# Where a scan leaves its result, and when its product with C is taken: a two-layer Mamba and expert block on one core

## The chip, the cores and the metric

The kernel runs on 1 core of one Trainium2 chip. The metric is the device time of one execution in microseconds; three executions before the change took 4998.74, 5000.21 and 5006.12 us, so the median is 5000.21 us. The profile is one further execution.

Five engines matter below: TensorE (PE; its weight loads are PEld), VectorE (DVE), ScalarE (ACT), GpSimd (POOL) and SyncE (SP), which here only issues DMAs. Each works through its own queue in order. SBUF and PSUM are the two memories on the core: TensorE writes to PSUM, the tiles of the loads lie in SBUF.

## The reference, cut to what matters

The input is (2, 256, 64, 64): two batches of 256 channels and 4096 positions. Layer 0 is a Mamba block over the positions, with 256 inner channels. Layer 1 is a layer norm, two Mamba blocks (one forward, one over the flipped sequence, 512 inner channels each), and then a mixture of 8 experts weighted by a softmax. The part that the change touches is the state recurrence, the same in all three Mamba blocks, with 16 states to a channel:

```python
A = -jnp.exp(A_log)
dA = jnp.exp(dt[..., None] * A)
dBu = dt[..., None] * Bm[:, :, None, :] * xs[..., None]
def combine(c1, c2):
    a1, b1 = c1
    a2, b2 = c2
    return (a1 * a2, a2 * b1 + b2)
_, hs = jax.lax.associative_scan(combine, (dA, dBu), axis=1)
y = jnp.einsum('blds,bls->bld', hs, Cm) + xs * Dvec
y = y * jax.nn.silu(z)
return y @ out_proj_w.T
```

For every channel and state, h(t) = dA(t) h(t-1) + dBu(t). The states are multiplied by C(t) and summed over the 16 states; the skip xs * D is added, and the gate silu(z) multiplies.

## The kernel before

**Tiling.** The 4096 positions are cut into chunks of T = 512. Six jobs (2 batches x layer 0, layer 1 forward, layer 1 flipped) of 8 chunks each run one after the other. In a chunk, each block of 128 channels is worked in 4 groups of states; one such group of one block is a *quad*: a tile `bq` of 128 partitions (32 channel rows x 4 states) by 4 x 512. There are 640 quads. `QN` = 8 quads make one *period*; `n` is the quad's place in it (0 to 7). A quad has two halves `h` = 0 and 1, each of 2 x 512 elements; one half is one *slot*, so a period has 16 slots and the whole has 1280.

**What a quad goes through.**
- `emit_b` (line 742, GpSimd): b = dt*x times B into `bq`, 128x2048. Both inputs, `rxdt` and `bc`, lie in SBUF. It is emitted some three quads ahead. `bq` has six buffers.
- `emit_decay` (line 752, ScalarE): the decays `da` = exp(dt*A) of one half into PSUM, two activations. `da` has two buffers. Ahead of it, `emit_join` (line 763) folds the carried state into the first column of the second row of b, so that one scan can run over both rows.
- `emit_scan` (line 778, VectorE): the scan over 1024 elements, with `da` and `bq` as inputs. Its result goes over `da` in PSUM, except where `on_pool(g, h)` holds: there it goes over `bq` in SBUF.
- The product with C. Where `on_pool` holds (quads 0, 2 and 5 of a period, and the first half of quad 4 in every second period) GpSimd does it: `emit_times_c_quad` (lines 802 and 803), after a small copy of the last column, in place on `bq`. Elsewhere, 760 of the 1280 halves, VectorE does it: `emit_times_c` (line 787), from `da` in PSUM and `bc` in SBUF into `bq`.
- `emit_carry` (line 797, ScalarE): copies the last column of each row into `h_state`, the state carried to the next chunk, in the halves that VectorE multiplies.
- `emit_sum` (line 811, TensorE): four matmuls add a quad's products over the states into `y` in PSUM; `emit_skip` (line 818) opens `y` with the skip, and `emit_gate` (line 824, VectorE) takes `y` times the gate. `y` has one buffer.

**Order.** The loop of lines 1105 to 1147 emits slot by slot, and `in_order` ties each engine to that order. `SUMS` (line 65) says in which slot which quads are summed; `POOL_AT` (line 66) which products GpSimd does at the start of which quad ("c0 b4" at n = 1: the product with C of quad 0, then b of quad 4, both counted from the period's start). In between stand the other steps of the chunks to come, which `Slots` holds by slot and queue: projections, convolution (line 544), softplus (line 594, and `xdt` on GpSimd, line 598), gate (line 624), layer norms, and the scales of the experts (lines 918 to 921, once).

**Experts.** `experts()` (line 927) plans ahead of time how many of the 128 pairs (16 chunks of the two batches with 8 experts each) fit into the slots of the scans, by a budget of TensorE's and ScalarE's work in each slot; `sums_in` tells it which slots the sums take. Those pairs (lines 992, 1001, 1005) leave their results in DRAM. The others run in a last stage after the scans (lines 1326, 1330, 1337, 1350), where the early results are also weighted and added (lines 1275, 1276).

The heart of the loop before the change:

```python
if slot:
    emit_carry(*divmod(slot - 1, 2))
emit_decay(*divmod(slot + 1, 2))
sl.run(slot, "act")
sl.run(slot, "dve0")
emit_scan(g, h)
if (n, h) in ((1, 0), (5, 0)) and done:
    emit_gate(*done.pop(0))
sl.run(slot, "dve")
if not on_pool(g, h):
    emit_times_c(g, h)
```

Of the kernel before, what the change touches and what calls it, by code (L numbers as in the profile page):

```python
# [50 lines left out]
T = 512  # L51
# [10 lines left out]

POOL_HALF = (4, 0)

SUMS = {(0, 0): (-1,), (2, 0): (0, 1), (4, 0): (2, 3), (6, 0): (4,), (7, 0): (5, 6)}
POOL_AT = {0: "b3", 1: "c0 b4", 2: "b5", 3: "c2 b6", 4: "b7", 5: "h4 b8", 6: "c5 b9", 7: "b10"}
HUGE = 1e37

# [68 lines left out]
def hybrid_kernel(ctx: ExitStack, tc: tile.TileContext, a: dict, out: bass.AP):  # L137
    nc = tc.nc
# [19 lines left out]
    def in_order():  # L158

        ins = nc.cur_bb.bb.instructions  # L160
        for x in ins[traced[0] :]:
            if x.engine in tail:
                tc.add_manual_dep(
                    x, tail[x.engine],
                    mybir.DependencyInfo(mybir.DependencyClass.NoSync, mybir.DependencyReason.DATA),
                    reason="in_order",
                )
            tail[x.engine] = x.name
        traced[0] = len(ins)
# [24 lines left out]
    with ExitStack() as st:  # L194
# [155 lines left out]
        steps = [(job, c) for job in jobs for c in range(NCH)]  # L350
# [318 lines left out]
        bq, da, y = {}, {}, {}  # L669
        pending, wanted = [], []  # L670

        def at(g):

            i, jp, n = quads[g]
            return i, 2 * jp + n // SG, n % SG
# [45 lines left out]
        def flush(slot):  # L721
            for p in list(pending):
                if p[0] <= slot and (p[1] if len(p[1]) > 1 else p[1][0]) in cks[p[3]]:
                    pending.remove(p)
                    p[2]()
# [42 lines left out]
        def on_pool(g, h):  # L768

            n = quads[g][2]  # L770
            return n in POOL_C or (n, h) == POOL_HALF and g // QN % 2

        def emit_scan(g, h):
            i, j, sg = at(g)
            job, c = steps[i]
            d = da[g, h].rearrange("p q t -> p (q t)")
            b = bq[g][:, 2 * h : 2 * h + 2, :].rearrange("p q t -> p (q t)")
            nc.vector.tensor_tensor_scan(  # L778
                b if on_pool(g, h) else d, d, b,
                job.h[:, j, sg, 2 * h : 2 * h + 1] if c else 0.0, ALU.mult, ALU.add,  # L780
            )

        def emit_times_c(g, h):

            i, j, sg = at(g)
            d, two = da[g, h], slice(2 * h, 2 * h + 2)
            nc.vector.tensor_tensor(  # L787
                bq[g][:, two, :], d,
                cks[i]["bc", 1, sg].rearrange("p (o t) -> p o t", o=1).to_broadcast([P, 2, T]), ALU.mult,
            )  # L790

        def emit_carry(g, h):

            i, j, sg = at(g)
            d, two = da.pop((g, h)), slice(2 * h, 2 * h + 2)
            if not on_pool(g, h):
                nc.scalar.copy(steps[i][0].h[:, j, sg, two], d[:, :, T - 1])  # L797

        def emit_times_c_quad(g, groups=SG):
            i, j, sg = at(g)  # L800
# [7 lines left out]
        def emit_sum(g):  # L808
            i, j, sg = at(g)
            for q in range(SG):  # L810
                nc.tensor.matmul(  # L811
                    y[i, j][q * CG : (q + 1) * CG, :], stack, bq[g][:, q, :],
                    start=False, stop=(sg == SG - 1),
                )

        def emit_skip(i, j):
            y[i, j] = ps_y.tile([P, T], F32, tag="y", name=f"y_{i}_{j}")
            nc.tensor.matmul(
                y[i, j], steps[i][0].diagonal[:, j, :], cks[i]["xc", j], start=True, stop=False
            )  # L820

        def emit_gate(i, j):
            sz = cks[i]["sz", j]
            nc.vector.scalar_tensor_tensor(sz, y.pop((i, j)), 0.5, sz, ALU.mult, ALU.mult)
# [102 lines left out]
        def experts():  # L927

            last = 2 * nq + 15
            banks = sorted(sl.banks, key=lambda r: r[0])  # L930

            def fits(slot):

                at = sum(b[0] <= slot for b in banks)
                both = banks[:at] + [(slot, slot + 1, 0)] + banks[at:]
                return all(
                    both[k - 3][1] + both[k][2] <= both[k][0] for k in range(max(3, at - 2), min(len(both), at + 4))
                    if at in range(k - 3, k + 1)
                )

            def sums_in(slot):
                n, h = divmod(slot % 16, 2)
                return 1.25 * len(SUMS.get((n, h), ())) + (1 if (n, h) in ((2, 0), (6, 0)) else 0)

            todo = [(at, b, c, e) for at, b, c in sorted(ready) for e in range(E)]
            behind = act_behind = 0.0
            times = [[], [], []]

            def follows(l):

                k, m = divmod(len(times[l]), KC)
                if k == len(todo):
                    return None
                waits = [(l - 1, k * KC + 1, 2)] if l else []
                if m:
                    waits.append((l, k * KC, 0))
                elif k:

                    waits.append((l, k * KC - 1, 6 if l == 0 and todo[k][-1] == 0 else 4))
                    if l < 2:  # L960
                        waits.append((l + 1, k * KC - 1, 0))
                if any(n >= len(times[w]) for w, n, _ in waits):
                    return None
                return max([todo[k][0] + 3] + [times[w][n] + d for w, n, d in waits])

            for slot in range(last):
                behind = max(0.0, behind) + sl.products.get(slot, 0) + sums_in(slot) - PE_ROOM
                act_behind = max(0.0, act_behind) + sl.acts.get(slot + 1, 0) - ACT_ROOM
                for l in (2, 1, 1, 0, 0):
                    at = follows(l)  # L970
                    if at is None or slot < at:
                        continue
                    if behind + 2 > PE_BEHIND or act_behind + 1.3 > ACT_BEHIND or not fits(slot):
                        break
                    banks.insert(sum(b[0] <= slot for b in banks), (slot, slot + 1, 0))
                    times[l].append(slot)
                    behind += 2
                    act_behind += 1 if l == 2 else 1.3
            put = [
                (*item[1:], [times[l][k * KC + m] for l in range(3) for m in range(KC)])  # L980
                for k, item in enumerate(todo) if (k + 1) * KC <= len(times[2])
            ]
            emit_experts(put)
# [120 lines left out]
        done = []  # L1104
        for g in range(nq):
            i, jp, n = quads[g]
            for h in range(2):
                slot = 2 * g + h
                sl.run(slot, "sp")
                flush(slot)  # L1110

                if (n, h) in ((2, 0), (6, 0)):
                    emit_skip(i, 2 * jp + n // SG)
                sl.run(slot, "pe")
                for m in SUMS.get((n, h), ()):
                    if g - n + m >= 0:
                        emit_sum(g - n + m)
                sl.run(slot, "pe2")
                if (n, h) in ((0, 0), (4, 0)) and g:
                    done.append(at(g - 1)[:2])  # L1120

                if slot:
# [4 lines that stand above are left out]
                sl.run(slot, "dve0")  # L1127
                emit_scan(g, h)

                if (n, h) in ((1, 0), (5, 0)) and done:  # L1130
                    emit_gate(*done.pop(0))
                sl.run(slot, "dve")
                if not on_pool(g, h):
                    emit_times_c(g, h)

                if h == 0:
                    for what in POOL_AT.get(n, "").split():
                        m = g - n + int(what[1:])
                        if what[0] == "c":
                            emit_times_c_quad(m)  # L1140
                        elif what[0] == "h":
                            if on_pool(m, 0):
                                emit_times_c_quad(m, SG // 2)
                        else:
                            want_b(m)
                sl.run(slot, "pool")
            in_order()
        emit_sum(g)
        emit_gate(i, steps[i][0].nj - 1)
        sl.run_all(2 * nq, 2 * nq + 24)  # L1150
# [3 lines left out]
    with ExitStack() as st:  # L1154
# [5 lines left out]
        n, x, y, acc, wts, wb, lt, w_dram = {}, {}, {}, {}, {}, {}, {}, {}  # L1160
# [278 lines left out]
        for at, (b, i, e) in enumerate(pairs):  # L1439
# [5 lines left out]
            h = layer(n[b, i], 0, e, f"{i}_{e}_{b}")  # L1445
# [136 lines left out]
```

## Time and profile before

| what | value |
|---|---|
| median of 3 executions | 5000.21 us |
| profiled execution, its own time | 5004.36 us |
| span of the profile | 5002.6 us |
| busy: PE | 4256.4 us (85%) |
| busy: VectorE | 4568.5 us (91%) |
| busy: ScalarE | 3617.3 us (72%) |
| busy: GpSimd | 4342.2 us (87%) |
| first scan to last scan | 58 to 4468 us |
| mean granted TensorE clock | 0.928 |

How to read it: the span is the time from the first to the last instruction of the profiled execution. Busy times are sums over instructions of one engine; engines overlap. The scans fill the first 4468 us; GpSimd has little to do after that. In rows of groups, a line of the kernel, an engine and an operation stand with "out<-in", the shape, the count, the summed busy time, the mean of one in ns, and the idle time just before them with what ended it. In the timeline a row has its start, its length, engine, line, operation and tiles. The scans write to `da` 760 times (664 with a carried state, 96 in first chunks) and to `bq` 520 times (456 and 64).

### The profile page before, as it was taken

The page shows a single profiled execution, that of the slowest core. Times are in us where ns is not written, and L with a number is a line of the kernel's source. Part 1 is how long each engine was busy: PE and PEld are TensorE (multiplying, and loading weights), DVE is VectorE, ACT ScalarE, POOL GpSimd, SP SyncE. Part 2 cuts the span into 40 slices and gives each one's busy share as a digit, 9 for nine tenths or more (in the row PEclk, how much of TensorE's full clock was granted, in tenths as well). Part 3 has the DMA queues.
Part 4 walks back from the last instruction along what each step waited for, and adds up shares of the span by engine and source line. Part 5 has one row for each costly group of instructions (what it writes and reads, how often), then busy time and mean ns, then how long its engine had stood idle before and what let it go on. Part 6 is the DMA issues. An engine that isn't in the chain of part 4 may idle for free. (4 is left out here: it accounts for less than half of the span.)

```text
span 5002.6 us, 47346 instructions
## 1 busy us (share of the span) xinstructions
PE 4256.4 (85%) x14912; PEld 1473.8 (29%) x14912; DVE 4568.5 (91%) x3097; ACT 3617.3 (72%) x7304; POOL 4342.2 (87%) x1424
## 2 busy tenths in 40 slices
PE   5777778778776899989999999889868999989999
PEld 1222222222222233333333333223222333334444
DVE  6998999999999999999999999999999999964655
ACT  5777777777777788877788788888767888862232
POOL 6998999999999999999999999999999999960000
PEclk8778899999887999999999999999989999999999
DMA  5455454444444555446776555555434455436643
GB/s 192 157 188 168 157 168 153 157 144 154 163 158 148 175 179 176 166 171 232 246 238 216 171 174 169 189 171 189 169 127 146 171 185 191 171 121 236 227 160 126
DMA packets 335408, 875.26 MB, mean 175 GB/s; under 512 B 36315, under 2 KB 111861, under 8 KB 293173
## 3 DMA queue, kind: packets, MB, share of 16 engines
q1 hardware_dynamic: 326164, 835.39, 48.3%
q0 software_dynamic: 8992, 36.85, 2.8%
q8 instruction: 118, 1.93, 0.2%
q14 instruction: 134, 1.09, 0.1%
HBM read 673.27 MB, written 198.84 MB: 174 GB/s over the span
## 5 line engine op out<-in xcount | busy, mean ns | idle before, releaser
L742 POOL TENSOR_TENSOR bq<-rxdt,bc 128x2048 f32<-128x2048 f32 x640 | 2894.3, 4545 | 15.7 <-DMA rxdt<-xdtd 7.7
L752 ACT ACTIVATE da<-rdt,w_a 128x512 f32<-128x512 f32 x2560 | 1756.9, 686 | 114.2 <-DVE bq L778 68.0
L778 DVE TENSOR_TENSOR_SCAN da<-da,h_state,bq 128x1024 f32<-128x1024 f32 x664 | 1558.0, 2346 | 60.4 <-ACT da L752 46.2
L803 POOL TENSOR_TENSOR bq<-bq,bc 128x2048 f32<-128x2048 f32 (+1 forms) x280 | 1180.4, 4216 | 22.6
L778 DVE TENSOR_TENSOR_SCAN bq<-da,h_state,bq 128x1024 f32<-128x1024 f32 x456 | 1059.7, 2338 | 22.0 <-ACT da L752 21.8
L811 PE MATMUL y<-bq,stack 128*32 128x512 f32 x5120 | 744.8, 667 | 254.3 <-POOL bq L803 229.5
L787 DVE TENSOR_TENSOR bq<-da,bc 128x1024 f32<-128x1024 f32 x760 | 926.4, 1219 | 15.7
L992 PE MATMUL e<-eh,ew 128*128 128x512 f32 x1376 | 669.8, 621 | 52.3 <-DVE sp L594 13.6
L797 ACT COPY h_state<-da 128x2 f32<-128x2 f32 x759 | 119.3, 157 | 631.6 <-DVE bq L787 628.3
L763 ACT ACTIVATE bq<-h_state,bq,a 128x1 f32<-128x1 f32 x1120 | 429.8, 384 | 2.9 <-POOL bq L742 2.3
L992 PEld LDWEIGHTS e<-eh,ew 128*128 128x128 f32 x1376 | 250.5, 194 | 466.5 <-issue 234.9
L458 PE MATMUL z<-nx,w_in 128*128 128x512 f32 x640 | 326.6, 639 | 62.5 <-DVE q L423 21.1
L811 PEld LDWEIGHTS y<-bq,stack 128*32 128x32 f32 x5120 | 140.7, 116 | 798.8 <-POOL bq L803 347.7
L531 PE MATMUL conv<-xs,w_conv 64*64 64x512 f32 x2560 | 346.6, 617 | 31.3 <-ACT xs L515 29.1
L992 PE MATMUL e<-en,ew 128*128 128x512 f32 x688 | 329.6, 612 | 26.9 <-DVE xr L891 16.1
L458 PE MATMUL xs<-nx,w_in 128*128 128x512 f32 x640 | 316.9, 622 | 34.7 <-DVE sz L624 20.7
L1330 ACT ACTIVATE h<-hp,of,sc 128x512 f32<-128x512 f32 x168 | 130.6, 778 | 277.5 <-PE hp L1326 274.7
L1005 ACT ACTIVATE eh<-e,of,sc 128x512 f32<-128x512 f32 x344 | 260.1, 769 | 53.9 <-PE e L992 53.6
L843 PE MATMUL o<-sz,w_out 128*128 128x512 f32 x640 | 295.7, 601 | 0.0
L598 POOL TENSOR_TENSOR xdt<-sp,xc 128x512 f32<-128x512 f32 x160 | 203.3, 1274 | 49.7 <-DVE sp L594 49.7
L778 DVE TENSOR_TENSOR_SCAN da<-da,bq 128x1024 f32<-128x1024 f32 x96 | 219.4, 2286 | 4.3 <-ACT da L752 2.3
L458 PEld LDWEIGHTS z<-nx,w_in 128*128 128x128 f32 x640 | 123.6, 202 | 266.3 <-issue 146.8
(145 smaller groups left out, 4762.3 us busy)
## 6 DMA issues: line engine op xcount, KB each, us to landing
rxdt<-xdtd SPq DMA_DIRECT2D x160, 1024.0 KB, 6.1
rdt<-dtd SPq DMA_DIRECT2D x160, 1024.0 KB, 6.8
bc<-bcd SPq DMA_DIRECT2D x384, 256.0 KB, 3.2
ew<-in_W SPq DMA_DIRECT2D x172, 256.0 KB, 4.5
u<-u SPq DMA_DIRECT2D x86, 512.0 KB, 5.7
u<-eu SPq DMA_DIRECT2D x82, 512.0 KB, 4.1
dtd<-sp SPq DMA_DIRECT2D x160, 256.0 KB, 3.3
xdtd<-xdt SPq DMA_DIRECT2D x160, 256.0 KB, 3.5
```

The lines of the kernel that those rows point to most:

```text
L458: nc.tensor.matmul(ps, job.matrices["in", half][:, k, j * P : (j + 1) * P], rhs, start=(k == 0), stop=(k == KC - 1),)
L531: nc.tensor.matmul(v[r][64 * col : 64 * col + 64, :], job.matrices["conv"][rows, 2 * jp + j, k, :], ck["xs", jp][rows, j, k : k + T] if k ...
L742: nc.gpsimd.tensor_tensor(bq[g], ck["rxdt", j], over_groups(ck["bc", 0, sg]), ALU.mult)
L752: nc.scalar.activation(da[g, h][:, k, :], cks[i]["rdt", j][:, q, :], AF.Exp, scale=steps[i][0].w["a"][:, j, q * SG + sg : q * SG + sg + 1],)
L763: nc.scalar.activation(bq[g][:, q, 0:1], job.h[:, j, sg, q : q + 1], AF.Identity, scale=cks[i]["a0", j][:, h, sg : sg + 1], bias=bq[g][:, ...
L778: nc.vector.tensor_tensor_scan(b if on_pool(g, h) else d, d, b, job.h[:, j, sg, 2 * h : 2 * h + 1] if c else 0.0, ALU.mult, ALU.add,)
L787: nc.vector.tensor_tensor(bq[g][:, two, :], d, cks[i]["bc", 1, sg].rearrange("p (o t) -> p o t", o=1).to_broadcast([P, 2, T]), ALU.mult,)
L803: nc.gpsimd.tensor_tensor(b, b, cks[i]["bc", 1, sg].rearrange("p (o t) -> p o t", o=1).to_broadcast([P, groups, T]), ALU.mult,)
L811: nc.tensor.matmul(y[i, j][q * CG : (q + 1) * CG, :], stack, bq[g][:, q, :], start=False, stop=(sg == SG - 1),)
L843: nc.tensor.matmul(v[m], job.w["out"][:, j, m * P : (m + 1) * P], ck["sz", j], start=False, stop=(j == job.nj - 1),)
L992: nc.tensor.matmul(ps, ew[l][:, k, m * P : (m + 1) * P], key[x][:, k, :], start=(k == 0), stop=(k == KC - 1),)
L1005: nc.scalar.activation(key[dst][:, m, :], key["ps", l, m], AF.Relu, bias=of[:, l, e, m : m + 1], scale=sc[:, l, e, m : m + 1],)
```

## The change

All scans write over b. In the 760 halves whose product with C belongs to VectorE, that product is now taken in place on `bq`, one slot later, behind the next scan; the carry copies from `bq`. Sums, skip and gate move by one slot, and so does what the planner of the experts is told of them.

```diff
-SUMS = {(0, 0): (-1,), (2, 0): (0, 1), (4, 0): (2, 3), (6, 0): (4,), (7, 0): (5, 6)}
+SUMS = {(0, 1): (-1,), (2, 1): (0, 1), (4, 1): (2, 3), (6, 1): (4,), (7, 1): (5, 6)}
...
             nc.vector.tensor_tensor_scan(
-                b if on_pool(g, h) else d, d, b,
+                b, d, b,
                 job.h[:, j, sg, 2 * h : 2 * h + 1] if c else 0.0, ALU.mult, ALU.add,
             )
...
         def emit_times_c(g, h):
             i, j, sg = at(g)
-            d, two = da[g, h], slice(2 * h, 2 * h + 2)
+            b = bq[g][:, 2 * h : 2 * h + 2, :]
             nc.vector.tensor_tensor(
-                bq[g][:, two, :], d,
+                b, b,
                 cks[i]["bc", 1, sg].rearrange("p (o t) -> p o t", o=1).to_broadcast([P, 2, T]), ALU.mult,
             )
         def emit_carry(g, h):
             i, j, sg = at(g)
-            d, two = da.pop((g, h)), slice(2 * h, 2 * h + 2)
+            two = slice(2 * h, 2 * h + 2)
             if not on_pool(g, h):
-                nc.scalar.copy(steps[i][0].h[:, j, sg, two], d[:, :, T - 1])
+                nc.scalar.copy(steps[i][0].h[:, j, sg, two], bq[g][:, two, T - 1])
...
-                return 1.25 * len(SUMS.get((n, h), ())) + (1 if (n, h) in ((2, 0), (6, 0)) else 0)
+                return 1.25 * len(SUMS.get((n, h), ())) + (1 if (n, h) in ((2, 1), (6, 1)) else 0)
...
-                if (n, h) in ((2, 0), (6, 0)):
+                if (n, h) in ((2, 1), (6, 1)):
                     emit_skip(i, 2 * jp + n // SG)
...
-                if (n, h) in ((0, 0), (4, 0)) and g:
+                if (n, h) in ((0, 1), (4, 1)) and g:
                     done.append(at(g - 1)[:2])
...
-                if (n, h) in ((1, 0), (5, 0)) and done:
+                if (n, h) in ((1, 1), (5, 1)) and done:
                     emit_gate(*done.pop(0))
                 sl.run(slot, "dve")
-                if not on_pool(g, h):
-                    emit_times_c(g, h)
+                if slot and not on_pool(*divmod(slot - 1, 2)):
+                    emit_times_c(*divmod(slot - 1, 2))
...
+        emit_carry(g, 1)
+        emit_times_c(g, 1)
         emit_sum(g)
```

## The prediction

> **What bounds the kernel now.** I read first where the time lies. The busy times of the stretch from the first scan to the last, 58 to 4468 us, and the page's costliest groups:
>
> ```profile
> 58.00:4468.00 4410.00, 3709.59 (x13528) 1237.31 (x13528) 4274.10 (x2782) 3441.57 (x7054) 4305.18 (x1375) 0.92 0.51 174
> ...
> L742 POOL TENSOR_TENSOR bq<-rxdt,bc 128x2048 f32<-128x2048 f32 x640 | 2894.3, 4545 | 15.7 <-DMA rxdt<-xdtd 7.7
> ...
> L778 DVE TENSOR_TENSOR_SCAN da<-da,h_state,bq 128x1024 f32<-128x1024 f32 x664 | 1558.0, 2346 | 60.4 <-ACT da L752 46.2
> L803 POOL TENSOR_TENSOR bq<-bq,bc 128x2048 f32<-128x2048 f32 (+1 forms) x280 | 1180.4, 4216 | 22.6
> ...
> L787 DVE TENSOR_TENSOR bq<-da,bc 128x1024 f32<-128x1024 f32 x760 | 926.4, 1219 | 15.7
> ```
>
> The first line gives length, then busy PE, PEld, DVE, ACT, POOL. VectorE works 4274 of 4410 us and GpSimd 4305: both bound the scan stage, and each can give at most some 105 to 136 us before the other holds. The 640 quads make 80 periods of 8 quads (16 slots): 4410 / 80 = 55.1 us a period, in which VectorE is busy 53.4 and GpSimd 53.8. The last stage (4470 to 5002.6) is TensorE's, 513 of 533 us busy.
>
> Next, what the product with C costs, in the order of time:
>
> ```profile
> 2511.99 2.36 DVE L778 TENSOR_TENSOR_SCAN da<-da,h_state,bq 128x1024 f32<-128x1024 f32 x1
> 2514.38 1.23 DVE L787 TENSOR_TENSOR bq<-da,bc 128x1024 f32<-128x1024 f32 x1
> ```
>
> From the scan's start to the product that reads it are 2.39 us; where something else follows a scan the step is 2.25 (129.48 to 131.73 below). So the product's dependence costs 0.13 us.
>
> Last, does VectorE do anything today with **both inputs in SBUF** while GpSimd works? L787 reads da from PSUM. The set-up of the scales (L918 to L921, 32 elements a partition) reads SBUF alone and falls into the scans. VectorE, then GpSimd at that time:
>
> ```profile
> 129.48 2.34 DVE L778 TENSOR_TENSOR_SCAN bq<-da,h_state,bq 128x1024 f32<-128x1024 f32 x1
> 131.73 0.66 DVE L594 SCALAR_TENSOR_TENSOR sp<-dt,sp 128x512 f32<-128x512 f32 x1
> 132.32 0.18 DVE L918 TENSOR_TENSOR sc<-sc,bn 128x32 f32<-128x32 f32 x1
> 132.42 4.52 DVE L919 TENSOR_TENSOR of<-bn 128x32 f32<-128x32 f32 x1
> 136.97 1.19 DVE L920 TENSOR_TENSOR of<-of,sc 128x32 f32<-128x32 f32 x1
> 138.20 1.19 DVE L921 TENSOR_TENSOR of<-of,bn 128x32 f32<-128x32 f32 x1
> ```
> ```profile
> 127.87 9.02 POOL L742 TENSOR_TENSOR bq<-rxdt,bc 128x2048 f32<-128x2048 f32 x2
> 136.85 2.48 POOL L598 TENSOR_TENSOR xdt<-sp,xc 128x512 f32<-128x512 f32 x2
> ```
>
> L918 takes 0.18 us, its twin L919 4.52: it ends at 136.94, when GpSimd's second product ends (127.87 + 9.02 = 136.89). L920 and L921 end within 0.07 us of the two xdt products. So such an operation waits for the whole GpSimd instruction that is running, and gets in at the next boundary (L918 hit the one at 132.38). The other direction, in the last stage:
>
> ```profile
> 4875.40 1.22 DVE L1275 TENSOR_TENSOR u<-u,wb 128x1024 f32<-128x1024 f32 x1
> 4876.65 3.26 DVE L1276 TENSOR_TENSOR x<-x,u 128x1024 f32<-128x1024 f32 x1
> ```
> ```profile
> 4875.57 3.25 POOL L1221 TENSOR_TENSOR nm<-nm,n 128x1024 f32<-128x1024 f32 x1 [60.29 <-DVE n L1206]
> ```
>
> GpSimd's operation takes 3.25 instead of 2.36 (L1211, alone, same size): it stands 0.90 behind L1275. L1276 then ends at 4879.91, 1.09 after GpSimd (4878.82). So the two exclude each other and take turns; a 128x1024 product holds GpSimd off 1.09 us.
>
> **The change, part by part.**
>
> *Scans write b instead of da* (760 of 1280; the others do already): 2346 against 2338 ns, -6 us on VectorE.
>
> *The product behind the next scan*: -0.13 x 760 = -99 us of VectorE's work. It comes due only while VectorE bounds.
>
> *Carry reads SBUF, not PSUM*: 760 copies of 157 ns (L797); the nearest copies from SBUF take 183 to 197 (L514, L517): at most +30 us of ScalarE, 78% busy here, nothing on the path. The copy also gets earlier: it waits 628 us for L787 today, in future for the scan alone, and da comes free with the scan. The 75 us that scans wait for da (L778's rows) may go: 0 to -75. A new wait: the product overwrites column T-1 and so waits for the carry, which stands first in ScalarE's slot, with the scan's 2.26 us between. Longest lateness of ScalarE today 3.9 us; all of VectorE would queue behind. Taken as 0.
>
> *Sums, skip, gate a slot later*: same count, TensorE 84% busy. Quad 0's sum now stands one slot before the quad that reuses its buffer, but GpSimd does a product with C (4.5 us) first; GpSimd waits 0.7 us for sums today. 0. Y's one PSUM buffer keeps its order: gate, skip and sums move together.
>
> *The plan of early experts* moves with the sums: the changed program issues 174 instead of 172 ScalarE operations of L1001, so one pair of 42 leaves the last stage: 24 matmul records, eight of L1350 taking 3.60 us in the timeline at 4878.5, = -11 us.
>
> *The last product after the loop*: one step of 1.1 us, 0.
>
> *The product now reads bq and bc, both SBUF.* Its own duration stays: 1219 (PSUM) against 1220 (L1275, two in SBUF). [...]
>
> But each product now takes its turn against GpSimd, which reads SBUF 98% of the stage. This is the whole price. Nothing shows it for such a stream, so bounds first. **Low**: GpSimd stands for each hold and nothing else is lost: 55.1 + 9.5 products x 1.09 = 65.5 us a period (9.5 = 760 / 80). **High**: each product waits out a whole GpSimd product of 4.51: VectorE 53.4 - 1.2 + 9.5 x 4.51 = 95. **Middle**: asked at a random moment it waits half, 2.25: 52.2 + 21.4 = 73.6.
>
> Better, replay one period by hand (scan step 2.26, product 1.13 with GpSimd again after 1.09, GpSimd 4.51, its small copy 0.24 ahead of a product with C, gate 0.59; b products run quads ahead). At 0 the scan of quad 0 starts, b3 has just begun and ends 4.47. The previous quad's product gets in there, to 5.60; second scan to 7.86. Only now may c0 start: to 12.61. Scans of quad 1 and the gate end at 12.97, 0.4 after b4 began: the product waits to 17.12. Then it alternates: b5 to 22.72, product to 23.85, second scan of quad 2 to 26.11, which c2 has awaited; c2 to 30.86. Quad 3's scans end 30.63, just in time for the boundary. Product, b6 to 36.46, product, b7 to 42.06, product, b8 to 47.66, product to 48.79, scan to 51.05, c5 to 55.80; quad 6's scans end 56.2, again just late, behind b9 (60.31). Product, b10 to 65.91, product, b11 to 71.51, product to 72.64, where the next quad 0 starts. GpSimd idles 3 times for its scans (3.4 + 3.4 + 3.4 us); VectorE waits 2 to 4 us for most turns. Two xdt (1.25 each) and every second period a half product with C (2.34) are not in it: up to 3.8 more, partly inside GpSimd's idle time; I add 1.4: **74 us**. Margins of 0.2 to 0.4 us decide whole 4.5 us turns, so 69 to 79.5.
>
> Sum: 80 x (74 - 55.1) = +1510, -11; the -99 and -75 are inside the replay. From the profiled span: 5002.6 + 1499 = 6502; the median lies 2.4 below that span (the profiled run was 5004.4): 6500.
>
> **Rivals.**
> *GpSimd alone bounds*: 65.5 us, 80 x 10.4 = +830, so 5820 (5700 to 6080). For it: b products run three quads ahead. Against: its queue is in order, and the products with C stand behind scans that now come late. Chance 0.10.
> *Each turn is lost*, because scans and GpSimd fall into step on the wrong side of the boundary: above 79.5, up to 95 us: 6950 to 8190. For: two margins above are just late. Against: a loser asks early for the next. 0.09. [...]
> *No turn-taking for this product* (the far side): the three places are coincidences of other waits. Then VectorE gains 99 + 6 and up to 75 of waits, GpSimd's idle 105 caps it at about 80: 5000 - 80 - 11 = 4910. It decides if a wait stays under 0.13 us a product. Against: L919's 4.52 for 32 elements. 0.03. *Not measurable*, gain and turns cancelling: 0.01. That the order isn't as named can be left aside: in the changed program each product stands behind the next scan, inputs bq and bc.
>
> **Numbers.** Forecast 0.77, own range 6110 to 6950. The rivals at 0.10 and 0.09 lie mostly outside, so the range is 6080 to 6950. A measurement tells 0.2% (10 us) from none: faster 0.03, same 0.01, slower 0.96.
>
> **What would show it.** L787's mean at 3 to 4 us instead of 1.22, ending at ends of GpSimd's instructions; L742's mean near 5.1 (its wait for a hold counted in); L802 waiting on scans far over today's 53 us; VectorE near 100% busy by such durations; ScalarE and TensorE the same work over a longer stage; the last stage 11 us shorter. Wrong if L787 stays at 1.2, or if GpSimd has no idle time (first rival).

## The result, and the profile after

The changed kernel takes 6396.56 us (median of 4, 6388.42 to 6396.84); before it is 4999.48 us here. The ratio is 1.2787, 95% interval 1.2765 to 1.2809: 28% slower. The profiled execution took 6396.84 us, its span is 6395.0 us.

The stages first: the windows of the scan stage and of the last stage of the changed kernel (length, then busy PE, PEld, DVE, ACT, POOL, then the granted clock, the DMA share and GB/s).

```profile
58.00:5860.00 5802.00, 4286.20 (x13505) 1330.42 (x13506) 5762.87 (x2777) 3478.15 (x7049) 4757.56 (x1374) 0.85 0.39 132
5870.00:6395.00 525.00, 504.59 (x1252) 220.97 (x1248) 276.40 (x274) 149.23 (x200) 28.88 (x41) 0.99 0.55 189
```

The scan stage ends at 5870 instead of 4470 us: 5812 / 80 = 72.7 us a period against 55.1. The last stage is 525 us against 533. All of the loss lies in the scans. There VectorE now counts as busy 99% of the time, GpSimd 82%. The costliest groups say of what kind this busy time is.

```profile
L742 POOL TENSOR_TENSOR bq<-rxdt,bc 128x2048 f32<-128x2048 f32 x640 | 3233.4, 5068 | 161.0 <-issue 78.6 <-PE y L811 73.4 <-DMA rxdt<-xdtd 6.7
L778 DVE TENSOR_TENSOR_SCAN bq<-da,h_state,bq 128x1024 f32<-128x1024 f32 x1120 | 2592.1, 2332 | 7.9 <-ACT da L752 7.6
L787 DVE TENSOR_TENSOR bq<-bq,bc 128x1024 f32<-128x1024 f32 x760 | 2472.0, 3253 | 2.8 <-ACT h_state L797 2.7
...
L797 ACT COPY h_state<-bq 128x2 f32<-128x2 f32 x760 | 142.7, 188 | 772.5 <-DVE bq L778 770.3
...
L802 POOL COPY h_state<-bq 128x4 f32<-128x4 f32 (+1 forms) x280 | 72.6, 259 | 650.9 <-DVE bq L778 650.9
```

The same 760 products with C went from 926 to 2472 us, 1.22 to 3.25 us each: +1546 us. A scan is unchanged at 2.33 us. GpSimd's b product went from 4.55 to 5.07 us, and its small copy, which waits for the scans of its quad, from 53 us of idle time to 651. The wait for the other engine stands inside the length of the instruction, so this profile counts it as busy: VectorE's 99% is here no measure of work. The granted TensorE clock is lower too (0.85 in the scan stage, 0.92 before), but the scans of VectorE keep their 2.33 us and TensorE is busy for 4286 of the 5802 us, so nothing points at it as the cause.

The timeline shows the wait. VectorE, then GpSimd, in a stretch in which every slot has a product:

```profile
3024.17 1.65 DVE L787 TENSOR_TENSOR bq<-bq,bc 128x1024 f32<-128x1024 f32 x1
3025.74 2.28 DVE L778 TENSOR_TENSOR_SCAN bq<-da,bq 128x1024 f32<-128x1024 f32 x1
3027.94 3.35 DVE L787 TENSOR_TENSOR bq<-bq,bc 128x1024 f32<-128x1024 f32 x1
3031.22 2.28 DVE L778 TENSOR_TENSOR_SCAN bq<-da,bq 128x1024 f32<-128x1024 f32 x1
3033.41 3.35 DVE L787 TENSOR_TENSOR bq<-bq,bc 128x1024 f32<-128x1024 f32 x1
3036.69 2.28 DVE L778 TENSOR_TENSOR_SCAN bq<-da,bq 128x1024 f32<-128x1024 f32 x1
3038.89 3.33 DVE L787 TENSOR_TENSOR bq<-bq,bc 128x1024 f32<-128x1024 f32 x1
```
```profile
3020.21 4.52 POOL L803 TENSOR_TENSOR bq<-bq,bc 128x2048 f32<-128x2048 f32 x1
3024.70 16.44 POOL L742 TENSOR_TENSOR bq<-rxdt,bc 128x2048 f32<-128x2048 f32 x3
```

The first product starts 0.56 us before GpSimd's L803 ends (3024.73) and takes 1.65, which is that wait and the usual 1.1. Then the two engines walk in step: three b products take 16.44 us, 5.48 each, where three took 13.52 in the kernel before:

```profile
2496.37 13.52 POOL L742 TENSOR_TENSOR bq<-rxdt,bc 128x2048 f32<-128x2048 f32 x3
```

One slot of VectorE takes 5.47 (3027.94 to 3033.41). The scan runs inside GpSimd's product, the product with C between two of GpSimd's. A turn of VectorE costs GpSimd 5.48 - 4.51 = 0.97 us; a turn of GpSimd costs VectorE what is left of the 4.51 us when the scan is done, here 3.35 - 1.2 = 2.1. The whole trace agrees: 686 of the 760 products take more than 1.25 us, and each of these ends 1.08 to 1.09 us after the end of a GpSimd instruction.

### The profile page after: what moved, and what is told of

Its sections match the earlier page's. It is cut to its first block, busy times and chain, and to the rows that moved or that the text cites. A ratio compares the mean times of both kernels' runs of the same rounds, so it can differ in the third digit from the quotient of the medians.

```text
span 6395.0 us, 47308 instructions
## 1 busy us (share of the span) xinstructions
PE 4831.1 (76%) x14912; PEld 1566.7 (24%) x14912; DVE 6067.2 (95%) x3098; ACT 3658.7 (57%) x7307; POOL 4798.1 (75%) x1425
## 4 chain that ended last, share of the span: by engine, by line
DVE 63%; issue 15%; PE 11%; ACT 7%; POOL 2%; DMA 2%; SPq 0%; DVEq 0%; POOLq 0%; ACTq 0%
DVE bq L778 32%; DVE bq L787 24%; PE hp L1328 4%; ACT da L752 3%; PE conv L531 2%; PE y L1352 2%; PE e L992 2%; DVE sz L624 1%; DVE xc L544 1%; DVE sz L824 1%; POOL bq L742 1%; PE y L811 1%; DVE sp L594 1%; ACT sp L590 1%; POOL bq L803 1%
## 5 line engine op out<-in xcount | busy, mean ns | idle before, releaser
L742 POOL TENSOR_TENSOR bq<-rxdt,bc 128x2048 f32<-128x2048 f32 x640 | 3233.4, 5068 | 161.0 <-issue 78.6
L778 DVE TENSOR_TENSOR_SCAN bq<-da,h_state,bq 128x1024 f32<-128x1024 f32 x1120 | 2592.1, 2332 | 7.9 <-ACT da L752 7.6
L787 DVE TENSOR_TENSOR bq<-bq,bc 128x1024 f32<-128x1024 f32 x760 | 2472.0, 3253 | 2.8 <-ACT h_state L797 2.7
L811 PE MATMUL y<-bq,stack 128*32 128x512 f32 x5120 | 1057.5, 693 | 877.9 <-DVE bq L787 809.3
L803 POOL TENSOR_TENSOR bq<-bq,bc 128x2048 f32<-128x2048 f32 (+1 forms) x280 | 1182.3, 4223 | 22.7 <-POOL h_state L802 0.2
L992 PE MATMUL e<-eh,ew 128*128 128x512 f32 x1392 | 770.4, 688 | 82.2 <-DVE xr L876 22.6
L797 ACT COPY h_state<-bq 128x2 f32<-128x2 f32 x760 | 142.7, 188 | 772.5 <-DVE bq L778 770.3
L802 POOL COPY h_state<-bq 128x4 f32<-128x4 f32 (+1 forms) x280 | 72.6, 259 | 650.9 <-DVE bq L778 650.9
L598 POOL TENSOR_TENSOR xdt<-sp,xc 128x512 f32<-128x512 f32 x160 | 291.2, 1821 | 247.8 <-DVE sp L594 238.6
L778 DVE TENSOR_TENSOR_SCAN bq<-da,bq 128x1024 f32<-128x1024 f32 x160 | 360.5, 2272 | 1.4 <-ACT da L752 1.4
L818 PE MATMUL y<-xc,w_d 128*128 128x512 f32 x320 | 196.1, 699 | 105.9 <-DVE sz L824 99.2
```

The costliest lines, as they stand in the source:

```text
L598: nc.gpsimd.tensor_tensor(v["xdt"], v["dt"], ck["xc", j], ALU.mult)
L742: nc.gpsimd.tensor_tensor(bq[g], ck["rxdt", j], over_groups(ck["bc", 0, sg]), ALU.mult)
L778: nc.vector.tensor_tensor_scan(b, d, b, job.h[:, j, sg, 2 * h : 2 * h + 1] if c else 0.0, ALU.mult, ALU.add,)
L787: nc.vector.tensor_tensor(b, b, cks[i]["bc", 1, sg].rearrange("p (o t) -> p o t", o=1).to_broadcast([P, 2, T]), ALU.mult,)
L803: nc.gpsimd.tensor_tensor(b, b, cks[i]["bc", 1, sg].rearrange("p (o t) -> p o t", o=1).to_broadcast([P, groups, T]), ALU.mult,)
L811: nc.tensor.matmul(y[i, j][q * CG : (q + 1) * CG, :], stack, bq[g][:, q, :], start=False, stop=(sg == SG - 1),)
```

## The experiments

The theory is turn-taking: a VectorE operation with two inputs in SBUF and a GpSimd operation that reads SBUF exclude each other for a whole instruction (here the 4.51 us of GpSimd's product, the 0.97 us of VectorE's turn). Rivals: the product's new place in the order (it waits for the carry; sums and gate come later); a scan that writes into SBUF, or work in place, is slow in itself; two SBUF sources are slow in themselves.

**e1_same_slot: the operands without the order.** Before, with these edits; the carry moves into the slot too, ahead of the product.

```diff
-                b if on_pool(g, h) else d, d, b,
+                b, d, b,
...
-                bq[g][:, two, :], d,
+                b, b,
```

> The operands alone: scans write b and the product is taken in place from SBUF, but in its old place, in the slot of its own scan; sums, skip, gate and the planner as before the change. Turn-taking between VectorE's product with two SBUF inputs and GpSimd's products: L787 means 3 to 3.5 us and the time is 6350 to 6700 us, about the changed kernel's 6397 plus the product's wait for its own scan and carry. If the later place in the order costs the time (its wait for the carry, sums and gate a slot late): about 5000 to 5250 us, L787 at 1.2 us. If a result in SBUF or an operation in place is slow in itself: about 6400 us as well, so this run does not part that from turn-taking.

6396.32 us, ratio 1.2791 (1.2772 to 1.2811), the changed kernel's time. The product's group in its profile:

```profile
L787 DVE TENSOR_TENSOR bq<-bq,bc 128x1024 f32<-128x1024 f32 x760 | 2143.8, 2821 | 309.7 <-ACT h_state L797 309.4
```

It stands 310 us for the carry, which the later place avoids (2.8 us in the changed kernel), but waits that much less for GpSimd: 2144 + 310 = 2454 us against 2472 + 3. The place in the order made no difference in either direction; the new operands alone, scans into SBUF among them, cost as much as the whole change.

**e3_psum_operand: the order and the SBUF scans without the second SBUF input.** The changed kernel, with the decays of the slot's own scan in place of the scan's result; the output leaves out the scan's result in these halves.

```diff
+            last = min(2 * g + h + 1, 2 * nq - 1)
             nc.vector.tensor_tensor(
-                b, b,
+                b, da[divmod(last, 2)],
```

> The changed kernel, except that the product takes the decays of the scan just done (PSUM) in place of the scan's result: one SBUF input instead of two, everything else the same, scans in SBUF, the order, the carry it waits for, the same writes. The scan's results are thus left out of the output in these halves. Turn-taking: L787 back at 1.2 us, L742 at 4.54 us, time 4890 to 5000 us (VectorE is relieved of 0.13 us a product, GpSimd bounds at 4305 of the 4410 us of the scan stage). If the order, the carry or scans into SBUF cost the time: about 6400 us. If two SBUF sources are slow in themselves, without GpSimd: also 4890 to 5000 us.

4992.06 us, ratio 0.9981 (0.9971 to 0.9991). Both groups of its profile are back:

```profile
L742 POOL TENSOR_TENSOR bq<-rxdt,bc 128x2048 f32<-128x2048 f32 x640 | 2893.7, 4542 | 39.8 <-issue 18.6 <-PE y L812 14.0 <-DMA rxdt<-xdtd 6.9
...
L788 DVE TENSOR_TENSOR bq<-da,bc 128x1024 f32<-128x1024 f32 x760 | 916.4, 1206 | 15.0 <-ACT h_state L798 14.8
```

One operand moved from SBUF to PSUM takes away the whole loss, with the order, the carry and the scans into SBUF left as they are. Beside that it is 0.2% faster than the kernel before, some 10 us. In the two profiles most of this lies in the scans (the last scan ends 9 us earlier), and about 2 us in the last stage. Its scan stage is 4407 us long, of which GpSimd works 4303. This is not quite the change without the exclusion: the product now holds `da`, so ScalarE waits 411 us for it, and the scans still wait 98 us for their decays, as before (75) and not as in the changed kernel (9).

**e4_pool_writes: two SBUF inputs beside a GpSimd that only writes.** The output leaves out b, and C in GpSimd's halves.

```diff
-            nc.gpsimd.tensor_tensor(bq[g], ck["rxdt", j], over_groups(ck["bc", 0, sg]), ALU.mult)
+            nc.gpsimd.memset(bq[g], 0.001)
...
-            nc.gpsimd.tensor_tensor(
-                b, b, ...
+            nc.gpsimd.memset(b, 0.001)
```

> The changed kernel, but GpSimd only writes: its products b and its products with C become fills with a constant, so that it reads SBUF only for xdt (the output leaves out b, and C in GpSimd's halves). VectorE's product keeps its two SBUF inputs. Turn-taking of two readers: L787 at 1.2 us except beside xdt, VectorE alone bounds at 52 us a period, 4700 to 4850 us. If the exclusion covers GpSimd's writes too: L787 waits for each fill, between 1.2 and 3.3 us by the fill's length. If two SBUF sources or working in place are slow in themselves: L787 stays at 3.25 us, about 6300 us.

4913.85 us (0.9828, 0.9809 to 0.9848). A product of VectorE and a fill of GpSimd, from the two timelines:

```profile
2012.80 1.22 DVE L787 TENSOR_TENSOR bq<-bq,bc 128x1024 f32<-128x1024 f32 x1
```
```profile
2013.23 1.80 POOL L742 MEMSET bq<- 128x2048 f32 x1 [2.96 <-PE y L808]
```

The fill begins 0.43 us after the product. The product takes 1.22 us, and the fill 1.80, as the one at 2008.46 does, beside which no product runs. Over all 760, the product's mean is 1.21 us, with both inputs in SBUF and in place. With one input in PSUM it was 1.22 in the kernel before and 1.21 in e3. So neither two SBUF sources nor work in place cost anything in themselves here, and GpSimd's fills did not hold VectorE off. What is left is its reads. The xdt products, the only ones of GpSimd in these scans that still read SBUF, still pay: 1.75 us in the mean instead of 1.27, and each of the 86 that take over 1.4 us ends 1.12 to 1.14 us after a product of VectorE. The time is 64 us above the 4700 to 4850 that I expected: VectorE alone leaves a stage of 4330 us, not 4200. It is busy for 4214 of them and waits above all for ScalarE (56 us for decays, 57 for the `thx` of the convolution).

**e5_split_pool: more ends.** The changed kernel, with each product of GpSimd in two of half the size.

```diff
-            nc.gpsimd.tensor_tensor(bq[g], ck["rxdt", j], over_groups(ck["bc", 0, sg]), ALU.mult)
+            for two in (slice(0, 2), slice(2, 4)):
+                nc.gpsimd.tensor_tensor(
+                    bq[g][:, two, :], ck["rxdt", j][:, two, :],
+                    ck["bc", 0, sg].rearrange("p (o t) -> p o t", o=1).to_broadcast([P, 2, T]), ALU.mult,
+                )
...
```

The products with C are cut in the same way.

> The changed kernel, but each of GpSimd's 128x2048 products is issued as two of 128x1024 (2.34 us each): same work, twice as many ends at which VectorE can get its turn. Turn-taking: a product waits at most 2.34 us, some 1.2 in the mean; VectorE 52.2 + 9.5 x 1.2 = 64 us a period, GpSimd 53.8 + 11.5 x 0.15 + 9.5 x 0.97 = 65; with some misfit 65 to 68 us, time 5790 to 6030 us, L787 at 2.0 to 2.6 us. If the cost lies in VectorE's product, the carry or the order: 6397 us or more, for GpSimd's work only grows, by some 140 us.

5819.97 us, ratio 1.1641 (1.1623 to 1.1658), 577 us less than the changed kernel although GpSimd issues 880 products more (1800 instead of 920).

```profile
L743 POOL TENSOR_TENSOR bq<-rxdt,bc 128x1024 f32<-128x1024 f32 x1280 | 3476.4, 2746 | 11.2 <-DMA rxdt<-xdtd 6.8 <-issue 3.1 <-PE y L816 0.7
...
L791 DVE TENSOR_TENSOR bq<-bq,bc 128x1024 f32<-128x1024 f32 x760 | 1593.7, 2097 | 41.2 <-ACT h_state L801 41.1
```

The product's wait falls from 2.04 to 0.89 us. Its scan stage is 5232 us, 65.4 a period, of which GpSimd is busy 5171: with short instructions it is GpSimd that bounds, by its work and the turns it gives. Its small copy, one SBUF input of four elements, takes its turn too: with a median of 0.19 us, it lasts 1.21 at 2503.11, until the product of VectorE that began at 2501.89 ends.

**e6_half_turns: fewer turns.** As e3, but in first halves only (`b, b if h else da[divmod(last, 2)]`): 400 turns instead of 760. The output leaves out the scan's result in first halves.

> The changed kernel with the product's scan result replaced by the decays in PSUM (as in e3_psum_operand) in first halves only; second halves, 400 of the 760, keep both inputs in SBUF. First halves thus leave the scan's result out of the output. Turn-taking priced by the turn: 5 turns a period in place of 9.5, at the 2.0 us of wait each that the changed kernel shows (L787 3.25 less 1.21): VectorE 52.2 + 5 x 2.0 = 62 us a period, GpSimd at least 55.1 + 5 x 0.97 = 60: 5390 to 5600 us. If a turn mattered only where turns follow each other (the misfits of the replay), below 5390; if the loss did not go by turns, the kernel stays above 5900.

5647.53 us, ratio 1.1296 (1.1276 to 1.1317), 47 us above the expected stretch. In one kernel and one stage the same line then has two lengths: 3074 ns in the mean for the 400 with two SBUF inputs, and 1204 ns in the median for the 360 that read PSUM (the second row has minimum, median and maximum in ns):

```profile
L788 DVE TENSOR_TENSOR bq<-bq,bc 128x1024 f32<-128x1024 f32 x400 | 1229.8, 3074 | 11.1 <-ACT h_state L798 11.0
...
L788 DVE TENSOR_TENSOR bq<-da,bc x360: 1189/1204/1225, 65.8 to 5108.2; 128x1024 f32<-128x1024 f32 x180
```

The 400 wait 1.87 us each, 745 us in all, and the kernel loses 649: 1.6 us for a turn, against 1397 / 760 = 1.8 in the changed kernel. The loss goes by turns, to within an eighth.

**e7_carry_act and e8_carry_act_small: looking for a faster kernel.** Since e3 puts the bound on GpSimd, e7 gives the 280 small copies of GpSimd to ScalarE, in the kernel before the change; e8 also puts line 544's steps behind the scan.

```diff
-            if not on_pool(g, h):
-                nc.scalar.copy(steps[i][0].h[:, j, sg, two], d[:, :, T - 1])
+            src = bq[g][:, two, :] if on_pool(g, h) else d
+            nc.scalar.copy(steps[i][0].h[:, j, sg, two], src[:, :, T - 1])
...
-            nc.gpsimd.tensor_copy(steps[i][0].h[:, j, sg, :groups], b[:, :, T - 1])
...
-                sl.run(slot, "dve0")
                 emit_scan(g, h)
+                sl.run(slot, "dve0")
```

> The kernel before the change, but ScalarE copies the carried state of GpSimd's halves too (520 more copies of 0.16 to 0.19 us) and GpSimd's 280 copies of 0.215 us, 0.06 us apart from the product, are gone. e3 showed that relief of VectorE alone brings nothing because GpSimd works 4305 of the 4410 us of the scan stage; here GpSimd gets 77 us less. If GpSimd bounds: 4925 to 4975 us. If VectorE (4274 us) with its waits for ScalarE's decays bounds, or ScalarE's 99 us more delay the decays: 4985 to 5040 us.

> As e7_carry_act, and VectorE's 160 steps of the convolution (L544) stand behind the slot's scan instead of ahead of it, so that they fill the 0.13 us that a product loses right behind its own scan. At most 9.5 of 16 of the 160 hit such a slot: 95 x 0.13 = 12 us less than e7 where VectorE bounds, nothing where GpSimd does; slower than e7 if TensorE's next projection waits for the convolution's result.

Both are slower than before: 5026.84 us (1.0055, 1.0041 to 1.0069) and 5069.48 us (1.0141, 1.0127 to 1.0155). The group of GpSimd's products with C in e7, where before the copy had waited 53 us for scans:

```profile
L802 POOL TENSOR_TENSOR bq<-bq,bc 128x2048 f32<-128x2048 f32 (+1 forms) x280 | 1200.8, 4288 | 150.7 <-ACT h_state L797 146.7
```

GpSimd now waits 147 us for a copy that stands in ScalarE's queue. Over the scan stage of the two profiles it works 52 us less than before (4253 us of 4432, before 4305 of 4410) and idles 74 us more. In e8 the wait for the copy is 189 us. No kernel that I ran computes the whole reference and beats the one before.

Not tried: the new order with the scan's result left in PSUM. The product would then hold `da` one slot longer, and what that costs with two buffers no run shows.

## Why the prediction was right

**The mechanism** was read off three places of the trace of before, and it held: e3 and e4 each take away one side of the exclusion (VectorE's second SBUF input, GpSimd's reads) and each takes away the loss (4992 and 4914 us).

**The size.** The forecast was 74 us a period, measured are 72.7; that is the 104 us between 6500 and 6397. VectorE's sum by the measured wait is 52.2 + 9.5 x 2.04 = 71.6 of the 72.7; the middle estimate had the wait at 2.25, half of a GpSimd product.

That the replay's own 72.64 comes so near is in part luck. It opens with b3 just begun and closes when b11, the b3 of the next period, is done: nine b products in a period that has eight. Carried on by its own rules, the next round is 2.2 us shorter, for its first product finds GpSimd idle and the second scan ends after 5.65 us instead of 7.86: 70.4 us. It also charges 1.09 us for a turn that costs GpSimd 0.97, and it leaves out the softplus, convolution and gate steps of VectorE (lines 594, 544, 624). In the trace of the changed kernel a period, counted from first scan to first scan, takes 64.2 to 86.5 us. The 36 with neither xdt nor half products, the case of the replay, take 72.1 us in the mean (68 to 78), the other 43 take 73.3. So the replay came out near its case by errors that cancel, and the term that was too large is the 1.4 us for the steps outside it: with them the mean of the 79 periods is 72.8 us, 0.7 more than 72.1. Single periods spread widely, as the margins of 0.2 to 0.4 us let one expect.

**The steps at nothing.** The wait for the carry is 2.7 us in all; the copy from SBUF takes 188 instead of 157 ns, +23 us on ScalarE; sums, skip and gate cost nothing that VectorE waits for (`y` 1.8 us), but GpSimd's wait for them, 0.7 us and taken as nothing, became 73 us (the row of L742), in an engine that idles anyway. The last stage gave 8 us, forecast 11. The scans' wait for the decays fell from 75 to 9 us, as it might.

**The gain that was meant** is there and worth nothing. The product follows the next scan after 2.26 us, without the 0.13 us more that it lost behind its own. In the changed kernel the wait for GpSimd swallows this (e1, without it, takes the same time), and without the exclusion (e3) GpSimd's 4303 of 4407 us leave 0.2% of it. My price for the far rival, 4910 us, lies 80 us below e3. It let VectorE's relief run up to GpSimd's idle time, and in e3 that idle time stays. How much of the 80 us is due to e3's longer hold of `da` is not shown.

**The rivals.** GpSimd as the bound, 65.5 us a period, is not this kernel (72.7, with GpSimd idle 651 us for scans), but e5 comes out there (65.4). The rival of lost turns, above 79.5, came in six single periods (82.7 to 86.5 us), not in the mean.

## What to carry to other kernels

Before an operand is moved from PSUM to SBUF on VectorE, count its SBUF inputs: with two of them, beside GpSimd's products of SBUF tiles, it waited here for the end of the one that was running, 2.04 us in the mean where they take 4.5 us and 0.89 where they take 2.34. The price went by the length of that instruction, not by the operation's own 1.2 us. One or two stray operations of that kind in the old trace, a 32-element product that takes 4.5 us, were enough here to price a stream of them. Where such a stream can't be avoided, cut the other engine's instructions: halves gave back 577 of the 1397 us here.

## What the runs showed that I had not expected

When GpSimd's small copies are gone (e7), its b products take 4.62 us in the mean instead of 4.55, and its products with C 4.29 instead of 4.22. This looks like 66 us of slower work over 920 products, but no time is lost in it. 180 of these records are over 4.7 us long, and such a record begins some 0.4 us before the one ahead of it has ended:

```profile
865.48 4.92 POOL L802 TENSOR_TENSOR bq<-bq,bc 128x2048 f32<-128x2048 f32 x1
869.97 13.91 POOL L742 TENSOR_TENSOR bq<-rxdt,bc 128x2048 f32<-128x2048 f32 x3
```

The first ends at 870.40, the three b products at 883.88. From end to end the three take 13.48 us, 4.49 each, as before (13.52 for three). So a mean length alone does not show that an engine works more slowly; the distance from end to end does.
